# A conditioned transformer block on one core: sums and P7 issued later in a step, the second norm spread over four slots, other banks and buffers

## The chip, the cores and the metric

The kernel runs on one core of a Trainium2 chip. A core has five engines with queues of their own: TensorE (PE, matrix products), VectorE (DVE), ScalarE (ACT), GpSimd (POOL) and SyncE (SP), which here only issues DMAs. The metric is the device time of one execution in microseconds.

Before the change three runs took 2557.16, 2556.14 and 2556.53 us: the median is 2556.53 us.

## The reference

x is a tensor of 4 x 1024 tokens with 512 features, conditioned by a vector per sequence. In short (names as in the reference):

```python
def _tc_rmsnorm(x, t, gw, gb, bw, bb):
    g = (t @ gw.T + gb)[:, None, :]
    b = (t @ bw.T + bb)[:, None, :]
    inv_rms = jax.lax.rsqrt(jnp.mean(x * x, axis=-1, keepdims=True) + EPS)
    return g * x * inv_rms + b
...
# _attention: 16 heads of 32, softmax over 1024 keys, no mask
attn = jnp.einsum('blhd,bmhd->bhlm', q, k) / scale
p = jax.nn.softmax(attn, axis=-1)
o = jnp.einsum('bhlm,bmhd->blhd', p, v).reshape(B, L, D)
...
def _swiglu(x, gate_w, hid_w, out_w):      # 2048 hidden features
    return jax.nn.silu(x @ gate_w.T) * (x @ hid_w.T) @ out_w.T
...
h = x + _attention(_tc_rmsnorm(x, t, g1w, g1b, b1w, b1b), Wq, Wk, Wv, Wo)
block = h + _swiglu(_tc_rmsnorm(h, t, g2w, g2b, b2w, b2b), gate_w, hid_w, out_w)
return x + block
```

## The kernel before

Everything is float32 (the shift of the softmax travels in three bfloat16 parts). Features lie on the 128 partitions and tokens along the free axis. The 4096 tokens are 8 blocks (NBLK) of 512. Most products of PE are four at a time on 32 columns of weights each (`mm` with `columns[0] = DH`).

**Slots and rounds.** The main loop runs over slots g = 0 to 267. In slot g < 256 one round of attention begins: four heads, 256 queries and 256 keys (`scores`, L299). Four rounds (UN = 4) make one softmax j; `kind = g % 4` is the place in it. A round goes through the engines over several slots:
- `keep` copies the scores from their bank to SBUF on ACT (L306); `running_max` follows the maximum on DVE (L311).
- In a slot of kind 0, `max_T` and `parts` turn and reduce the maximum of the last four rounds; in kind 1 `parts_T` brings it back to rows (copy to mT on ACT, L338), and `spread` (L346) brings it to all keys: two products, each evicted by ACT to `shift`.
- `shifted` adds the shift (DVE, L352), `exponential` is on ACT (L355), `weighted` multiplies with the values (PE, L365, bank "av"), and `accumulate` adds the exponentials to one tile by a DMA on POOL's queue (L379).
- `fold_sum` (DVE) adds the two halves, `sums` (PE, L397) adds over the keys, `sums_out` copies the total (ACT, L406) and writes a compact form to DRAM (`compact`, L149, a DMA on ACT's queue). A step later `take` reads it as 128 x 8 numbers, `invert` takes the reciprocal, `put` (L165, ACT's queue) writes it back, and `sums_in` spreads it (SP's queue, L171). `normalize` multiplies.

**Feed-forward.** From g = 60 (FS) each slot pair also does half of a pass p = (g-60)//2: 128 hidden features of gate and of value for one block of 512 tokens. Gate and value products of one pass are made by a scheme with seven half-size products P1 to P7 (instead of eight) on sums of tokens (`token_sums`) and sums of weights (`weight_sums`, made in the first stage and kept in DRAM as s_w). P1 and P5 of the next pass are at the end of an odd slot (`pair_15`, `take_5`, `add_15`), P2 and P6 at the start of an even one (`pair_26`, then `copy_156`, L543, on ACT), then comes a **filling chain** (`filler`: the output product of an older pass, 32 matmuls of 512 columns, "pc"), P7 and `sub_5` (L550), in the next slot P3, the gate (`gate_tanh`, L560, `gate`), P4 and `hidden`. Passes 104 to 127 run in a tail loop behind slot 267.

**What sets the order.** On PE, DVE, ACT and POOL the order is that of the code. On SP, which issues most loads, a scheduler sets it. The first slots (g < 60) fill PE with projections from a queue of chains (`chain`), whose weights are loaded by `fetch` when the chain before is taken. A block of 32 slots (BS) also carries, for the block of tokens whose attention has ended: the load of the residual (slot 6 of a block, 1 MB), the output projections (slot 13 on, `project_out`, L443), the second norm (`norm_squares`, `norm_root`, the compact inverse by ACT's queue, `norm_scale`, `norm_mod`, L185, slots 15 to 25) and the token sums (25 to 27). These are hung into the loop by `after`, `between` and `amid` (end of a slot, before its end, in its middle).

**Banks and buffers.** PSUM: "sc" (scores), "av" (values), two of "w" (everything else), "wb" (bank_b of a pass). In SBUF tags that matter here: "fw" (4 buffers, weights of the projections and of the passes), "st" (2, staging of projected keys, queries and values once the token sums exist, and P5), "ow" (4, output weights), "inv", "tot", "rec".

Of the kernel before, what the change touches and what calls it, by code (L numbers as in the profile page):

```python
# [10 lines left out]
F32 = mybir.dt.float32  # L11
# [6 lines left out]
P = 128  # L18
NB = 512
# [5 lines left out]
def tile_cond_transformer_block(  # L25
# [24 lines left out]
    HQ = 256  # L50
# [52 lines left out]
    def mm(dst, w, moving, start: bool, stop: bool, seeded: bool = False):  # L103
        n = columns[0]
        for k in range(0, P, n):
            nc.tensor.matmul(  # L106
                dst[k : k + n, :], w[:, k : k + n], moving, start=start, stop=stop, skip_group_check=seeded
            )
# [4 lines left out]
    bank_a, bank_b, fifth = {}, {}, {}  # L113
    state = {}
    turn = [1]

    def bank(name: str):

        turn[0] += 1
        if "sums" not in state and turn[0] % 3 == 0:  # L120
            return ps_b.tile([P, NB], F32, tag="wb", name=name)
        return ps.tile([P, NB], F32, tag="w", name=name)
# [13 lines left out]
    def norm_root(tag: str, inside: bool = False):  # L136
        if inside:
            pm = ps_av.tile([P, NB], F32, tag="av", name=f"pm{tag}")
        else:
            pm = ps.tile([P, NB], F32, tag="w", name=f"pm{tag}")  # L140
        mm(pm, ones_mean, state.pop(tag), True, True)
        inv = sb.tile([P, NB], F32, tag="inv", name=f"inv{tag}", bufs=1)
        nc.scalar.activation(inv, pm, AF.Sqrt, bias=eps)
        state[tag] = inv

    def compact(tag: str, t, rows: int, n: int):

# [45 lines left out]
    def norm_sum(dst, tag: str):  # L193

        pm = ps.tile([P, NB], F32, tag="w", name=f"pm{tag}")
        for c in range(C):
            sq = sb.tile([P, NB], F32, tag="h", name=f"sq{tag}_{c}", bufs=7)
            nc.scalar.activation(sq, dst[:, c, :], AF.Square)
            nc.tensor.matmul(pm, ones_mean, sq, start=(c == 0), stop=(c == C - 1))
        inv = sb.tile([P, NB], F32, tag="inv" if tag == "a0_0" else "tot", name=f"inv{tag}", bufs=1)  # L200
        nc.scalar.activation(inv, pm, AF.Sqrt, bias=eps)
        nc.vector.reciprocal(inv, inv)
        state[tag] = inv
# [15 lines left out]
        y[b, half] = t  # L219

    def load_wkq(hg: int):
        t = sb.tile([P, 2, C, P], F32, tag="fw", name=f"wkq{hg}", bufs=4)
        nc.sync.dma_start(out=t, in_=kq_w[hg])
        wkq[hg] = t

    def staging(name: str):

        if "sums" in state:
            return sb.tile([P, NB], F32, tag="st", name=name, bufs=2)
        return sb.tile([P, NB], F32, tag="h", name=name, bufs=7)  # L230


# [234 lines left out]

    def weight_sums(f: int, step: int):
        if step == 0:
            state["gh", f] = sb.tile([P, 2, C, P], F32, tag="fw", name=f"gh{f}", bufs=4)  # L470
            nc.sync.dma_start(out=state["gh", f], in_=gh_w[f])
        else:
            t = state.pop(("gh", f))
            a11, a12, a21, a22 = (t[:, i, k : k + 2, :] for i in range(2) for k in (0, 2))
            o = sb.tile([P, 4, 2, P], F32, tag="fw", name=f"s{f}", bufs=4)
            nc.vector.tensor_tensor(o[:, 0], a21, a22, ALU.add)
            nc.vector.tensor_tensor(o[:, 1], o[:, 0], a11, ALU.subtract)
            nc.vector.tensor_tensor(o[:, 2], a11, a21, ALU.subtract)
            nc.vector.tensor_tensor(o[:, 3], a12, o[:, 1], ALU.subtract)
            nc.sync.dma_start(out=s_w[f], in_=o)  # L480
# [18 lines left out]

    def load_f(p: int, part: int):  # L500
        f = p % NF
        fw[p, part] = sb.tile([P, 4, 2, P], F32, tag="fw", name=f"fw{p}_{part}", bufs=4)
        if part == 0:
            nc.sync.dma_start(out=fw[p, 0][:, 0:2], in_=gh_w[f][:, 0].rearrange("p (a c) o -> p a c o", a=2))
            nc.sync.dma_start(out=fw[p, 0][:, 2:4], in_=s_w[f][:, 0:2])
        else:
            nc.sync.dma_start(out=fw[p, 1][:, 0:2], in_=s_w[f][:, 2:4])
            nc.sync.dma_start(out=fw[p, 1][:, 2], in_=gh_w[f][:, 1, 2:4])
# [11 lines left out]
        product(a[:, RIGHT], fw[p, 0][:, 2], state["sums"][:, 0])  # L520

    def take_5(p: int):
        fifth[p] = sb.tile([P, HQ], F32, tag="st", name=f"p5_{p}", bufs=2)
        nc.scalar.copy(fifth[p], bank_a[p][:, RIGHT])

    def add_15(p: int):
# [73 lines left out]
    def between(g, fn, *a):  # L600
        halfway.setdefault(g, []).append((fn, a))

    def after(g, fn, *a):
        ended.setdefault(g, []).append((fn, a))
# [40 lines left out]
    for n in range(NBLK):  # L645
        g0 = (n + 1) * BS
        pin(g0 + 6, load_res, n)
        go = g0 + (13 if n < NBLK - 1 else 8)
        for d in range(C):
            first.append((go, None, project_out, (n, d)))  # L650
            pin(go - 3 + (d // 2 * 4 if n else 0), load_wo, n, d)
        if n < NBLK - 1:
            tag = f"f{n}"
            after(g0 + 16, add_res, n)
            for k in range(2):
                after(g0 + 15 + k, lambda n=n, tag=tag, k=k: norm_squares(x2[n], tag, k))
            if g0 + 17 < FS:
                between(g0 + 17, norm_root, tag)
            else:
                amid.setdefault(g0 + 17, []).append((norm_root, (tag, True)))  # L660
            between(g0 + 17, norm_compact, tag)
            after(g0 + 19, take, tag)
            between(g0 + 20, invert, tag)
            after(g0 + 21, put, tag)
            after(g0 + 22, norm_spread, tag)
            for c in range(C):
                after(g0 + 24 + c // 2, lambda n=n, tag=tag, c=c: norm_scale(x2[n], tag, c))
                after(g0 + 24 + c // 2, lambda n=n, c=c: norm_mod(1, n // QB, x2[n], c))
            after(g0 + 25, token_sums, n, 0)
            for i in range(1, 3):  # L670
                after(g0 + 26, token_sums, n, i)
            between(g0 + 27, token_sums, n, 3)
    for m in range(NBLK * C):
        if m:
            for qh in range(NB // HQ):
# [8 lines left out]
    def fetch():  # L684

        if loads:
            load, a = loads.popleft()
            load(*a)
# [11 lines left out]
    with tc.manual_schedule(  # L700
# [6 lines left out]
        wv[0] = sb.tile([P, C, D], F32, tag="b", name="wv", bufs=2)  # L707
        nc.sync.dma_start(out=wv[0], in_=v_w)
        load_modw(1)
        fetch()  # L710
        norm_sum(y[0, 0], "a0_0")

# [28 lines left out]
        def filler(p: int, tail: bool = False):  # L741
# [15 lines left out]
                (lambda: take_contract(q, pp)),  # L757
            )

        while g < END:  # L760
            kind = g % UN
            r_x, r_v = g - UN - 1, g - UN - 2
# [31 lines left out]
            if v_on:  # L794
                weighted(r_v)
                accumulate(r_v)
            if kind == 0 and n_on:
                sums(j_n)
                if j_n >= direct:
                    inverse(j_n)  # L800
                    normalize(j_n)
            if kind == 1 and m_on:
                spread(j_m, 2)
                mT.pop(j_m)
# [1 line left out]
                shifted(r_x, slice(HG // 2, HG))  # L806
            if g < NR:
                keep(g)
            if kind == 0 and n_on and j_n < direct:
                sums_out(j_n)  # L810
            if kind == 1 and n_on and near(j_n) and j_n < direct:
                nc.vector.reciprocal(state["rec", j_n], state["rec", j_n])
            if kind == 2 and n_on and not near(j_n):
                take(f"s{j_n}")
            if kind == 0 and o_on and not near(j_o):
                put(f"s{j_o}")
            if kind == 1 and s_on:
                take_av(j_s)
            due = bool(first) and first[0][0] <= g
            if not ffn:  # L820
                if x_on:
                    exponential(r_x)
                evict = chain(g, FG)
                if g < NR:
                    running_max(g, 0)
                    running_max(g, 1)
# [21 lines left out]
            elif even:  # L848
                load_f(p + 1, 1)
                pair_26(p)  # L850
                copy_156(p)
                if x_on:
                    exponential(r_x)
                if kind == 0 and m_on:
# [7 lines left out]
                    running_max(g, 1)  # L862
                if evict is not None:
                    evict()
                if kind == 0:
                    pair_7(p)
                    sub_5(p)
                for fn, a in halfway.pop(g, []):
                    fn(*a)
            else:  # L870
                load_f(p + 2, 0)
                extra = due or len(queue) > FG
                if kind == 3:
                    if extra:
                        chain(g)()
                    pair_7(p)
                    sub_5(p)
                pair_3(p)
                if kind == 1 and extra:
                    chain(g)()  # L880
                if kind == 3:
                    gate_tanh(p)
                if x_on:
# [4 lines left out]
                    fn(*a)  # L888
                if kind == 1:
                    gate_tanh(p)  # L890
                if g < NR:
                    running_max(g, 0)
                if kind == 3:
                    gate(p)
                if g < NR:
# [1 line left out]
                add_15(p + 1)  # L897
                if kind == 1:
                    gate(p)
                if kind == 3 and s_on:  # L900
                    fold_sum(j_s)
                pair_4(p)
# [15 lines left out]
        assert not (pinned or amid or halfway or ended or queue or first)  # L918
        n = NBLK - 1
        squares = []  # L920
        for c, tag in enumerate(("rmax", "shift", "tot", "inv")):
            sq = sb.tile([P, NB], F32, tag=tag, name=f"sqf{n}_{c}", bufs=1)
            nc.scalar.activation(sq, x2[n][:, c, :], AF.Square)
            squares.append(sq)
# [84 lines left out]
```

## Time and profile before

| | us |
|---|---|
| median of three runs | 2556.53 |
| profiled execution | 2552.28 |
| its span | 2550.5 |
| PE busy | 2412.4 (95%) |
| DVE busy | 1853.8 (73%) |
| ACT busy | 1404.3 (55%) |
| DMA moved | 509.68 MB, mean 200 GB/s |

The page divides the span into forty slices of 63.8 us. DVE and ACT fall in the last five, in which the tail loop runs:

```profile
DVE  2677877766868887788788877888788868833332
ACT  3666767765656665665566556665565656512110
DMA  5598999998878998888788978899788978863442
```

In such a line a digit is the busy share of a slice in tenths. A row of the costliest groups has the line, the engine, output and inputs, how often it ran, and then its busy time, the mean of one in ns, and the idle time of its engine just before, with what ended it. In the timeline, a row shows start and duration in us, and in brackets how long the engine had idled before it and which instruction released it. [...] The mean granted clock of PE was 0.989 of full speed.

### The profile page before, as it was taken

Reading aid. Unit: us, or ns where it says so; the run is one execution under the profiler, and the core shown is the slowest. Engines: PE = TensorE matmul, PEld = TensorE weight load, DVE = VectorE, ACT = ScalarE, POOL = GpSimd, SP = SyncE. Lnnn points to the kernel's source line nnn. Section 1 sums busy time; section 2 is a strip of 40 time slices with the busy share of each in tenths; the row PEclk is TensorE's granted clock in tenths of the full one; section 3 lists DMA queues with packets and bytes.
Section 4 is the critical chain, followed back from the end, with each engine's and each line's share of the span. In section 5 each row is a group of like instructions: output and inputs, shape, how many; then the busy total and the mean of one; then the engine's idle time right before and its main releaser. Section 6 shows DMA issues by size and latency. Waiting matters only on the chain. (4 is left out here: it accounts for less than half of the span.)

```text
span 2550.5 us, 71967 instructions
## 1 busy us (share of the span) xinstructions
PE 2412.4 (95%) x31749; PEld 1137.8 (45%) x31749; DVE 1853.8 (73%) x2180; ACT 1404.3 (55%) x1486; POOL 172.4 (7%) x207
## 2 busy tenths in 40 slices
PE   8989999998999999999999999999999999989999
PEld 3333333344444444444444444454445444434444
DVE  2677877766868887788788877888788868833332
ACT  3666767765656665665566556665565656512110
POOL 0000000000000000000000000000000000000000
PEclk9999999999999999999999999999999999999999
DMA  5598999998878998888788978899788978863442
GB/s 200 162 260 244 249 239 250 239 219 197 190 183 205 220 224 193 197 207 219 190 207 205 224 189 201 195 228 219 184 202 216 225 182 202 199 159 116 138 126 90
DMA packets 245085, 509.68 MB, mean 200 GB/s; under 512 B 44483, under 2 KB 125471, under 8 KB 217382
## 3 DMA queue, kind: packets, MB, share of 16 engines
q0 software_dynamic: 28656, 208.68, 42.4%
q1 hardware_dynamic: 197520, 295.66, 35.8%
q8 instruction: 251, 4.11, 0.6%
q10 hardware_dynamic: 18598, 0.74, 0.5%
q14 instruction: 60, 0.49, 0.1%
HBM read 253.87 MB, written 42.42 MB: 116 GB/s over the span
## 5 line engine op out<-in xcount | busy, mean ns | idle before, releaser
L352 DVE TENSOR_TENSOR raw<-raw,shift 128x2048 f32<-128x2048 f32 (+1 forms) x320 | 592.7, 1853 | 120.9 <-ACT shift L347 115.8
L355 ACT ACTIVATE raw<-raw 128x2048 f32<-128x2048 f32 x256 | 490.7, 1917 | 120.2 <-DVE raw L352 84.9
L306 ACT COPY raw<-sc 128x2048 f32<-128x2048 f32 x256 | 479.3, 1872 | 136.4 <-PE sc L299 102.1
L311 DVE TENSOR_TENSOR rmax<-rmax,raw 128x1024 f32<-128x1024 f32 x384 | 468.4, 1220 | 60.2 <-ACT raw L306 54.7
L106 PE MATMUL pc<-h,ow 128*32 128x512 f32 x4096 | 467.9, 593 | 2.1 <-DVE rec L419 2.1
L106 PE MATMUL pa<-x,fw 128*32 128x256 f32 x6144 | 387.3, 384 | 9.5 <-DVE x L448 5.7
L365 PE MATMUL av<-raw,v 128*32 128x256 f32 x4096 | 277.9, 389 | 28.3 <-ACT raw L355 21.9
L379 POOL DMA_DIRECT2D raw<-raw x192 | 165.3, 861 | 2059.6 <-ACT raw L355 1014.5
L299 PE MATMUL sc<-q,k 32*128 32x256 f32 x4096 | 295.2, 402 | 1.0 <-ACT raw L306 1.0
L106 PEld LDWEIGHTS pa<-x,fw 128*32 128x32 f32 x6144 | 198.5, 111 | 161.4 <-issue 24.2
L106 PE MATMUL pa<-sums,fw 128*32 128x256 f32 x4096 | 270.3, 380 | 0.0
L106 PE MATMUL pkq<-y,wkq 128*32 128x512 f32 (+1 forms) x1664 | 236.0, 605 | 14.9 <-DMA wkq<-in_kq_w 10.8
L299 PEld LDWEIGHTS sc<-q,k 32*128 32x128 f32 x4096 | 185.9, 185 | 138.1 <-issue 86.5
L106 PEld LDWEIGHTS pc<-h,ow 128*32 128x32 f32 x4096 | 127.6, 110 | 246.1 <-issue 217.6
L543 ACT COPY pb<-pa 128x256 f32<-128x256 f32 x128 | 46.0, 359 | 246.8 <-PE pa L106 179.3
L365 PEld LDWEIGHTS av<-raw,v 128*32 128x32 f32 x4096 | 107.8, 110 | 154.5 <-ACT raw L355 49.0
L106 PEld LDWEIGHTS pa<-sums,fw 128*32 128x32 f32 x4096 | 138.1, 111 | 84.9 <-issue 2.0
L560 ACT ACTIVATE t<-pa 128x512 f32<-128x512 f32 x128 | 77.8, 608 | 157.6 <-PE pa L106 157.5
L581 DVE SCALAR_TENSOR_TENSOR res<-pc,res 128x512 f32<-128x512 f32 x128 | 88.1, 688 | 82.7 <-PE pc L106 82.7
L106 PE MATMUL pb<-x,fw 128*32 128x256 f32 x2048 | 134.1, 379 | 9.9 <-ACT pb L543 9.9
L106 PEld LDWEIGHTS pkq<-y,wkq 128*32 128x32 f32 (+1 forms) x1664 | 74.1, 119 | 146.5 <-issue 122.9
L106 PE MATMUL pb<-sums,fw 128*32 128x256 f32 x2048 | 134.1, 379 | 2.8 <-DVE pb L550 2.8
(103 smaller groups left out, 1930.0 us busy)
## 6 DMA issues: line engine op xcount, KB each, us to landing
raw<-raw POOLq DMA_DIRECT2D x192, 1024.0 KB, 8.9
fw<-sw SPq DMA_DIRECT2D x256, 256.0 KB
ow<-in_out_w SPq DMA_DIRECT2D x128, 256.0 KB
fw<-in_gh_w SPq DMA_DIRECT2D x128, 256.0 KB
wkq<-in_kq_w SPq DMA_DIRECT2D x32, 512.0 KB
v<-vs SPq DMA_DIRECT2D x128, 128.0 KB
fw<-in_gh_w SPq DMA_DIRECT2D x128, 128.0 KB
k<-kqs SPq DMA_DIRECT2D x124, 128.0 KB
```

Source lines behind the costliest of these rows:

```text
L106: nc.tensor.matmul(dst[k : k + n, :], w[:, k : k + n], moving, start=start, stop=stop, skip_group_check=seeded)
L299: nc.tensor.matmul(sc[:, i, k, :], keys[rows, k * P : (k + 1) * P], queries[rows, :], start=True, stop=True)
L306: nc.scalar.copy(raw[r].rearrange("p k h q -> p h k q"), state.pop(("sc", r)))
L311: nc.vector.tensor_tensor(rmax[j], rmax[j], raw[r][:, k, :, :], ALU.max)
L352: nc.vector.tensor_tensor(t, t, s.unsqueeze(1).to_broadcast(list(t.shape)), ALU.add)
L355: nc.scalar.activation(raw[r], raw[r], AF.Exp)
L365: nc.tensor.matmul(av[j][i * DH : (i + 1) * DH, :], v[m, u][:, k, i * DH : (i + 1) * DH], raw[r][:, k, i, :], start=(kt == 0), stop=(kt == ...
L379: nc.gpsimd.dma_start(out=acc[j].rearrange("p k h q -> p (k h q)"), in_=raw[r].rearrange("p k h q -> p (k h q)"), accum_op=ALU.add,)
L543: nc.scalar.copy(bank_b[p][:, RIGHT], bank_a[p][:, RIGHT])
L560: nc.scalar.activation(state["t", p], bank_a[p], AF.Tanh, scale=0.5)
L581: nc.vector.scalar_tensor_tensor(r, pp, 0.5, r, ALU.mult, ALU.add)
```

## The change

1. **Sums.** `sums`, `sums_out` and `put` move, in slots of kind 0, from before (and around) `keep` to a new function `take_sums`. In g < 60 it is called behind the exponential and the chain, from g = 60 on behind P2, P6 and the copy of pb, before the exponential.
2. **P7.** `pair_7` and `sub_5` follow the filling chain in slots of kind 0 and of kind 2; before, those of kind 2 came at the start of slot kind 3.
3. **Second norm.** `norm_scale` stays in slots 24 and 25. `norm_mod` of features 0 and 1 goes to the end of slot 25, of 2 and 3 to the middle of slot 26; the token sums to the ends of 26, 26, 27 and 28. The norm's total and inverse share one tile.
4. **Output projections** of kind 1 slots go behind P1, P5 and the gate's tanh into a bank of the tag "av" (`spare_bank`), and are evicted behind the gate. In kind 3 the chain stays ahead of P3, but is evicted behind the first running maximum.
5. **Weights.** "fw" has five buffers, and one more `fetch` at the start puts the loads of the projection weights two steps ahead. Staging uses the four buffers of "ow" once the token sums exist; P5 has a tag of its own with two.

The number of instructions on each engine is the same. The core of the diff:

```diff
+    spare_bank = [False]
 
     def bank(name: str):
 
+        if spare_bank[0]:
+            spare_bank[0] = False
+            return ps_av.tile([P, NB], F32, tag="av", name=name)
...
-        mm(pm, ones_mean, state.pop(tag), True, True)
-        inv = sb.tile([P, NB], F32, tag="inv", name=f"inv{tag}", bufs=1)
-        nc.scalar.activation(inv, pm, AF.Sqrt, bias=eps)
-        state[tag] = inv
+        mm(pm, ones_mean, state[tag], True, True)
+        nc.scalar.activation(state[tag], pm, AF.Sqrt, bias=eps)
...
     def load_wkq(hg: int):
-        t = sb.tile([P, 2, C, P], F32, tag="fw", name=f"wkq{hg}", bufs=4)
+        t = sb.tile([P, 2, C, P], F32, tag="fw", name=f"wkq{hg}", bufs=5)
...
         if "sums" in state:
-            return sb.tile([P, NB], F32, tag="st", name=name, bufs=2)
+            return sb.tile([P, NB], F32, tag="ow", name=name, bufs=4)
...
     def take_5(p: int):
-        fifth[p] = sb.tile([P, HQ], F32, tag="st", name=f"p5_{p}", bufs=2)
+        fifth[p] = sb.tile([P, HQ], F32, tag="p5", name=f"p5_{p}", bufs=2)
         nc.scalar.copy(fifth[p], bank_a[p][:, RIGHT])
...
                 after(g0 + 24 + c // 2, lambda n=n, tag=tag, c=c: norm_scale(x2[n], tag, c))
-                after(g0 + 24 + c // 2, lambda n=n, c=c: norm_mod(1, n // QB, x2[n], c))
-            after(g0 + 25, token_sums, n, 0)
-            for i in range(1, 3):
-                after(g0 + 26, token_sums, n, i)
-            between(g0 + 27, token_sums, n, 3)
+            for c in range(2):
+                after(g0 + 25, lambda n=n, c=c: norm_mod(1, n // QB, x2[n], c))
+            for c in range(2, C):
+                between(g0 + 26, lambda n=n, c=c: norm_mod(1, n // QB, x2[n], c))
+            for i in range(4):
+                after(g0 + (26, 26, 27, 28)[i], token_sums, n, i)
...
+        fetch()
         fetch()
...
+        def take_sums(j: int, j_before: int):
+
+            if 0 <= j < NR // UN:
+                sums(j)
+                if j >= direct:
+                    inverse(j)
+                    normalize(j)
+                else:
+                    sums_out(j)
+            if 0 <= j_before < direct and not near(j_before):
+                put(f"s{j_before}")
...
-            if kind == 0 and n_on:
-                sums(j_n)
-                if j_n >= direct:
-                    inverse(j_n)
-                    normalize(j_n)
...
-            if kind == 0 and n_on and j_n < direct:
-                sums_out(j_n)
...
-            if kind == 0 and o_on and not near(j_o):
-                put(f"s{j_o}")
...
                 evict = chain(g, FG)
+                if kind == 0:
+                    take_sums(j_n, j_o)
                 if g < NR:
                     running_max(g, 0)
...
                 pair_26(p)
                 copy_156(p)
+                if kind == 0:
+                    take_sums(j_n, j_o)
                 if x_on:
                     exponential(r_x)
...
-                if kind == 0:
-                    pair_7(p)
-                    sub_5(p)
+                pair_7(p)
+                sub_5(p)
...
             else:
                 load_f(p + 2, 0)
                 extra = due or len(queue) > FG
-                if kind == 3:
-                    if extra:
-                        chain(g)()
-                    pair_7(p)
-                    sub_5(p)
+                evict = None
+                if kind == 3 and extra:
+                    evict = chain(g)
                 pair_3(p)
-                if kind == 1 and extra:
-                    chain(g)()
                 if kind == 3:
                     gate_tanh(p)
                 if x_on:
@@ -888,8 +894,13 @@
                     fn(*a)
                 if kind == 1:
                     gate_tanh(p)
+                    if extra:
+                        spare_bank[0] = True
+                        evict = chain(g)
                 if g < NR:
                     running_max(g, 0)
+                if kind == 3 and evict is not None:
+                    evict()
                 if kind == 3:
                     gate(p)
                 if g < NR:
@@ -897,6 +908,8 @@
                 add_15(p + 1)
                 if kind == 1:
                     gate(p)
+                    if evict is not None:
+                        evict()
```

More of the change, by code (lines that the diff above doesn't have):

```diff
@@ L199, in norm_sum @@
             nc.tensor.matmul(pm, ones_mean, sq, start=(c == 0), stop=(c == C - 1))
-        inv = sb.tile([P, NB], F32, tag="inv" if tag == "a0_0" else "tot", name=f"inv{tag}", bufs=1)
+        inv = sb.tile([P, NB], F32, tag="rmax" if tag == "a0_0" else "tot", name=f"inv{tag}", bufs=1)
         nc.scalar.activation(inv, pm, AF.Sqrt, bias=eps)
@@ L469, in weight_sums @@
         if step == 0:
-            state["gh", f] = sb.tile([P, 2, C, P], F32, tag="fw", name=f"gh{f}", bufs=4)
+            state["gh", f] = sb.tile([P, 2, C, P], F32, tag="fw", name=f"gh{f}", bufs=5)
             nc.sync.dma_start(out=state["gh", f], in_=gh_w[f])
@@ L474, in weight_sums @@
             a11, a12, a21, a22 = (t[:, i, k : k + 2, :] for i in range(2) for k in (0, 2))
-            o = sb.tile([P, 4, 2, P], F32, tag="fw", name=f"s{f}", bufs=4)
+            o = sb.tile([P, 4, 2, P], F32, tag="fw", name=f"s{f}", bufs=5)
             nc.vector.tensor_tensor(o[:, 0], a21, a22, ALU.add)
@@ L501, in load_f @@
         f = p % NF
-        fw[p, part] = sb.tile([P, 4, 2, P], F32, tag="fw", name=f"fw{p}_{part}", bufs=4)
+        fw[p, part] = sb.tile([P, 4, 2, P], F32, tag="fw", name=f"fw{p}_{part}", bufs=5)
         if part == 0:
@@ L920, in tile_cond_transformer_block @@
         squares = []
-        for c, tag in enumerate(("rmax", "shift", "tot", "inv")):
+        for c, tag in enumerate(("rmax", "shift", "tot", "oT0")):
             sq = sb.tile([P, NB], F32, tag=tag, name=f"sqf{n}_{c}", bufs=1)
```

## The prediction

> **What bounds the kernel now.** I read the shares of the page first, then the forty slices, then the sums of waits, then the timeline around each wait of TensorE (PE).
>
> ```profile
> PE 2412.4 (95%) x31749; PEld 1137.8 (45%) x31749; DVE 1853.8 (73%) x2180; ACT 1404.3 (55%) x1486; POOL 172.4 (7%) x207
> PE   8989999998999999999999999999999999989999
> PEclk9999999999999999999999999999999999999999
> ```
>
> PE is busy for 2412.4 of 2550.5 us, in every slice. No product is removed by the change, so it can win only PE's idle time (138 us) and the half-clock stretches that follow idle time. I laid PE's rows on the order in which the code issues them and took, for each group, its start minus the previous start minus the usual length of the previous group (0.86 us for a product on 32 columns, 0.43 for the sums, 3.43 for a chain of 512 columns). What is over is lost. Per block of 32 slots it is 33.5, 25.8, 34.5, 23.6, 25.9, 26.7, 24.1, 25.3 us; some 0.2 to 0.6 us a slot of that comes with every change of shape and stays. These rows say who is waited for:
>
> ```profile
> L106 PE MATMUL pkq<-y,wkq 128*32 128x512 f32 (+1 forms) x1664 | 236.0, 605 | 14.9 <-DMA wkq<-in_kq_w 10.8
> ```
> ```profile
> ACT pb L543 <- DMA res<-in_x: 16.1, 2, 8.1
> PEld sum L397 <- issue: 38.6, 34, 7.5
> PE sum L397 <- issue: 20.9, 11, 7.0
> ```
>
> **Part 1, weights two steps ahead.** At t = 132.26 PE waited 6.14 us for a wkq load and then ran the chain at half clock (64 matmuls took 9.24 us where 2 x 3.64 are usual). The slot of g=10 and the two after it lost 6.33 + 2.2 + 1.2 us. With one fetch more and a fifth "fw" buffer this load is issued a whole step earlier: I take 8 of 9.7. g=38 loses 3.93 us to the next such load: 3.9. At g=20 ACT sits in an inverse's DMA until a load lands (3.98 us, then 2.6 in the next slots); the DMA still waits, but the exponential now goes ahead of it: 2.5. The fifth buffer adds no transfer, but lets loads of all stages start earlier, among others that share the 16 DMA engines, which are busy 8 to 9 tenths in most slices; a load that is early takes its share from one that is due. I count that at nothing and hold 3 us either way for it. Bounds 5 to 19, taken 14.4.
>
> **Part 2, the sums behind P2 and P6.** The sum's product waits for the fold on DVE, and everything of PE behind it in the slot. Of 49 slots in the mixed stage these waits make 32.2 us: 3.65 and 7.22 at g=64 and 68, (part 4), some 13 us in slots 20 and 28 of the blocks (about 1.0 and 1.4 each), 0.13 in the others. Behind P2 and P6 the fold has 1.7 us more (two products), so waits up to that go: per block 1.0 (slot 20) + 0.8 (the small ones); slot 28 is counted in part 3. For g < 60 the sum goes behind the 3.43 us chain: the 0.96, 0.7, 0.7, 0.39 and smaller waits there, 4 us. Near the end (g=256 to 264) the sums wait 0.8 to 4.3 us: 3 of it goes. What moves to ACT: total (0.37), compact and put (0.5 and 0.3 to 0.4 us as issues) now stand between the copy of pb and the exponential, 1.2 us later for the exponential. ACT idles about 3.4 us before the mT copy in that slot, so it is hidden.
>
> It is not hidden where one of those DMAs waits. Each DMA on ACT's queue waits for the one that last used its completion semaphore (8 lanes, dealt in the order of building). In slot 4 of a block, that was in the trace the 1 MB residual:
>
> ```profile
> 1172.30 0.32 ACTq L165 DMA_DIRECT2D invss<-fews  x1
> 1172.66 0.36 ACT L543 COPY pb<-pa 128x256 f32<-128x256 f32 x1 [7.99 <-DMA res<-in_x]
> 1172.93 1.91 ACT L355 ACTIVATE raw<-raw 128x2048 f32<-128x2048 f32 x1
> 1173.07 1.07 PE L106 MATMUL pb<-x,fw 128*32 128x256 f32 x16 [2.75 <-ACT pb L543]
> ...
> 1174.74 0.34 ACT L338 COPY mT<-pt 12x256 bf16<-12x256 bf16 x1
> ...
> 1176.14 0.63 PE L346 MATMUL sp<-mT,select 12*128 12x256 bf16 x2
> ```
>
> ACT stands still for 8 us, and PE loses 2.75 us in P7. After the change the copy of pb is ahead, so P7 no longer waits. But the dealing shifts: put now follows the query load that is queued right behind the residual. These land at 908.0, 1176.2, 1445.9, 1715.1 and 1982.2 us in the trace; put went at 903.0, 1172.3, 1441.5, 1709.9 and 1977.3. Queued behind put on ACT are the exponential (1.91) and mT (0.34), and PE's spread waits for mT: it comes at landing + 0.35 + 1.91 + 0.35 + 0.1 = landing + 2.7, where it was put + 2.85 before (0.77 to P7, 0.86, 0.25, 0.97). So 4.5 us a block are lost more, 22.7 in five blocks, though P7's stall goes. PE then idles 6.7 us at a stretch (spread possible at 1172.2, comes at 1178.9).
>
> Here a rule bears. **The Trainium skill, "TensorE: Matmul & The Clock Gate", Part 1**: PE falls to half clock after about one idle window of 3.4 us, and gets the full clock back after a busy window. By it each 6.7 us stall costs one window at half speed, 1.7 us. The trace agrees only in part: 1.9 us of idle time was enough in slot 25, and 3.93 us at g=38 were not followed by a slow stretch. The nearest row is g=68, 7.2 us idle and then 0.4 + 0.84 + 1.03 + 0.64 = 2.9 us lost. By the rule 8.5 us, by the row 14.5, less 1.5 that slot 4 loses this way now: 7 or 13. I take 10. Slot 4: -33 (ends: 0 if the load lands early, -45).
>
> **Part 3, P7 behind the filling chain, and the norm over four slots.** In slot 25 mT stands behind two norm_mods on ACT:
>
> ```profile
> 1346.91 1.52 ACT L185 ACTIVATE x<-x,mod 128x512 f32<-128x512 f32 x2 [4.31 <-DVE x L182]
> 1348.34 0.34 ACT L338 COPY mT<-pt 12x256 bf16<-12x256 bf16 x1
> 1348.73 0.37 PE L346 MATMUL sp<-mT,select 12*128 12x256 bf16 x2 [1.72 <-ACT mT L338]
> ```
>
> They move to the end of slot 25 and the middle of 26, the token sums to 26 to 28. Gone: 1.9 in slot 25, 0.67 to 1.1 and 0.75 in 27 (P4 behind sub_5, which P7's place mends), 1.41 in 28: 4.4 to 5.2. The same DVE work lies now later, beside shifted (2.23), running_max (2 x 1.22) and the take_contract: I charge 1.3 for the exponential in 28 and up to 0.6 for P2, net 3.3. Four of six blocks have a half-clock stretch behind slot 25 (0.6 to 1.5): 0.7 a block on average. P7 moved by a step costs PE nothing, its inputs lie there; it waits for the copy of pb, issued a 3.43 us chain earlier.
>
> **Part 4, banks and buffers.** Output projections in the values' bank: slot 13 waited 1.03 + 1.0 us for DVE to empty the shared bank; av is idle then: 2.0 a block. The new bank could hold back the next av; that product is a step later, and the eviction (0.69) stands ahead: nothing, at worst 0.7 a block. That the second norm's total and inverse share one tile costs nothing: the root waits for the product that reads the total as it did. Staging moves from "st" to "ow" and take_5 gets its own tag:
>
> ```profile
> 627.37 0.37 ACT L524 COPY p<-pa 128x256 f32<-128x256 f32 x1 [7.17 <-DMA vs<-sv]
> ```
>
> Removed: 3.65 + 7.22 + 1.38 waits and 2.9 half clock = 15.2. New: the first output weights now wait for staging's stores; by the landings of the trace ow0 comes about 3.4 us after its first chain could start, and put and compact in that slot wait for ow2 and ow3. I charge 6; net 9 (ends 0 to 15).
>
> **The sum.** Blocks: 2.0 + 1.0 + 0.8 + 3.3 + 0.7 = 7.8, times 6 = 47. Then 18 (14.4 + 4) + 9 + 47 + 3 - 33 = 44. The profiled execution took 2552.28 us around a span of 2550.5; that is 4.25 us less than the median of the runs, 2556.53. 2552.3 - 44 = 2508, and with those 4 us **2512**.
>
> **Rivals.**
> - *The query load lands early* (PE is faster, the queue of SP gets its buffers sooner), so slot 4 loses nothing: 44 + 33 = 77, 2480. For it: SP's order is the scheduler's. Against it: the load stands behind 1 MB in all five blocks. 0.12.
> - *DVE becomes the bound.* It is at 8 tenths in most slices of the mixed stage. Then what is won in slots 13 and 24 to 28, 6 x (2.0 + 3.3 + 0.7) = 36, is lost again a step later: all of it gives 44 - 36 = 8 (2549), half of it 26 (2530). I put it at half, 2530. Against it: DVE's waits for PE and ACT (115.8 us for shift alone) are slack that later work can use. 0.2.
> - *The blocked ACT queue decides* (slower): compact and put in slot 4, in all blocks, wait for the residual and what follows it, and spread waits for them. All else gives 77, so it decides from 15.4 us a block (five blocks) or 11 (seven); put stood still for 8 us already now, but behind work that hid 5 of it. At 13 in seven blocks (8 more than now, and a block's half-clock stretch with it) it takes 91 from the 77: 2480 + 91 = 2571. 0.1, and 0.04 for an end within the bound of no change.
> - *The change doesn't do what it says* (the scheduler puts the loads back where they were, so part 1 gives nothing): 2526. It is inside the range, with the forecast in its 0.54.
>
> **How the numbers follow.** The likeliest is 2512, its own range 2496 to 2528. The range for 8 in 10 takes in DVE as a bound and half of the early load: 2488 to 2546. A difference under 0.2% (5 us) can't be told from none. Faster 0.86, same 0.04, slower 0.10.
>
> **What would show it.** Right: no wait for wkq at g=10; no wait of ACT's p for vs; in slot 25 spread at once behind sc; in slot 4 P7 without a wait, but spread waiting for mT some 6 us, and behind it a slow clock. Wrong: slot 4 without that wait (then about 2480), or av and P2 waiting for exponentials in slots 26 to 30 (DVE).

## The result and the profile after

The changed kernel takes 2525.52 us (median of four runs, 2524.23 to 2529.8), the kernel before 2556.34 us beside it: a ratio of 0.9884, with an interval of 0.9867 to 0.9901. That is 30.8 us or 1.2% faster; 44 us were forecast. The profiled execution of the changed kernel took 2529.8 us around a span of 2528.0 us, so it is the slowest of its four, and the spans of the two traces differ by 22.5 us only. What follows is summed against those 22.5.

First the page after: the shares of the engines, the clock and the row of the projections.

```profile
PE 2404.4 (95%) x31749; PEld 1131.5 (45%) x31749; DVE 1854.4 (73%) x2180; ACT 1409.2 (56%) x1486; POOL 172.8 (7%) x207
...
PEclk9999999999999999999999999999999999999999
...
L106 PE MATMUL pkq<-y,wkq 128*32 128x512 f32 (+1 forms) x1664 | 231.6, 594 | 6.6 <-ACT y L187 4.1
```

PE's idle time before the projections fell from 14.9 to 6.6 us, and loads no longer lead it. The mean granted clock, though, fell from 0.989 to 0.986: there is more half-clock time than before. The sums of waits after the change say where (waiting engine and line, what released it, us in total, times, longest):

```profile
ACT raw L357 <- DMA sumss<-total: 79.7, 19, 15.4
...
PE sp L348 <- ACT mT L340: 49.1, 8, 11.3
...
PEld sum L399 <- issue: 8.1, 23, 1.6
...
PE pma L106 <- ACT total L408: 4.7, 5, 1.7
```

PE's weight loads for the sums wait 8.1 us where it was 38.6, and the copy of pb no longer waits for the residual (16.1 us before). In their place stands a wait of 79.7 us on ACT, behind the issue of the compact sums, and PE waits 49.1 us for the mT copy in front of spread. This is slot 4 of a block, in the timeline of the changed kernel (start, duration, row; in brackets idle time before it, and releaser):

```profile
1141.17 0.33 SPq L435 DMA_DIRECT2D res<-in_x  x1
...
1141.59 0.39 SPq L290 DMA_DIRECT2D v<-vs  x1
1142.03 0.42 SPq L285 DMA_DIRECT2D q<-kqs  x1
...
1145.62 1.05 PE L106 MATMUL pb<-x,fw 128*32 128x256 f32 x16
...
1146.82 1.15 PE L301 MATMUL sc<-q,k 32*128 32x256 f32 x16
...
1153.41 0.50 ACTq L151 DMA_DIRECT2D sumss<-total  x1
1154.01 0.40 ACTq L167 DMA_DIRECT2D invss<-fews  x1
1154.45 1.91 ACT L357 ACTIVATE raw<-raw 128x2048 f32<-128x2048 f32 x1 [12.80 <-DMA sumss<-total]
1156.27 0.34 ACT L340 COPY mT<-pt 12x256 bf16<-12x256 bf16 x1
...
1156.66 0.58 PE L348 MATMUL sp<-mT,select 12*128 12x256 bf16 x2 [8.70 <-ACT mT L340]
```

P7 (the pb row) goes without a wait, as forecast. The total was there at 1141.65, but compact could be issued only at 1153.41. The trace records which semaphore a DMA raises and which an instruction waits for: compact waits for the one that the value load (issued 1141.59) raises, and put for that of the query load. Both loads stand behind the 1 MB residual, and by the records the last of their parts landed at 1153.34 and 1153.52. ACT takes its queue in order: the exponential has had its input from DVE since 1141.78 and starts at 1154.45, 0.04 us after put's issue ends. PE is idle from 1147.96 to 1156.66. What follows it is this table of stretches (their times and length, busy us of PE, PEld, DVE, ACT and POOL with counts, then granted clock, DMA share and GB/s):

```profile
1137.00:1147.00 10.00, 10.00 (x134) 4.96 (x138) 8.72 (x14) 2.71 (x4) 0.86 (x1) 1.00 0.70 181
1147.00:1156.60 9.60, 0.96 (x16) 0.63 (x16) 0.24 (x1) 2.15 (x2) 0.00 (x0) 0.81 0.91 251
1156.60:1163.40 6.80, 6.74 (x60) 2.71 (x63) 3.75 (x4) 4.32 (x6) 0.86 (x1) 0.52 0.94 169
1163.40:1170.00 6.60, 6.60 (x112) 3.43 (x104) 6.37 (x7) 4.63 (x6) 0.00 (x0) 1.00 0.61 193
```

In the 6.8 us after the stall the mean clock is 0.52. In finer stretches it is 0.50 from 1152.88 to 1163.12 and 1.00 just before and behind: PE is idle for the first 3.8 us of that and then works at half clock for 6.5 us, where the forecast had one window of 3.4 us.

The account by stage, from the start of one slot's scores to the next in both traces:

| stage | forecast, us | traces, us |
|---|---|---|
| ahead of slot 0 | 0 | +1.0 |
| slots 0 to 59 | -18 | -11.6 |
| slots 60 to 71 | -9 | -10.6 |
| slots 4 to 7 of five blocks | +33 | +10.9 +6.7 +6.3 +8.8 +9.5, in all +42.3 |
| all other slots from 72 to 251 | -47 | -40.0 |
| from slot 252 to the end | -3 | -3.6 |
| sum | -44 | -22.5 |

### The profile page after: what moved, and what is told of

Same layout as the page of the kernel before. It is cut to its first block, busy times and chain, and to the rows that moved or that the text cites. A ratio compares the mean times of both kernels' runs of the same rounds, so it can differ in the third digit from the quotient of the medians.

```text
span 2528.0 us, 72020 instructions
## 1 busy us (share of the span) xinstructions
PE 2404.4 (95%) x31749; PEld 1131.5 (45%) x31749; DVE 1854.4 (73%) x2180; ACT 1409.2 (56%) x1486; POOL 172.8 (7%) x207
## 5 line engine op out<-in xcount | busy, mean ns | idle before, releaser
L106 PEld LDWEIGHTS pa<-x,fw 128*32 128x32 f32 x6144 | 193.1, 111 | 166.4 <-issue 30.5
```

The lines of the kernel that those rows point to most:

```text
L106: nc.tensor.matmul(dst[k : k + n, :], w[:, k : k + n], moving, start=start, stop=stop, skip_group_check=seeded)
```

## The experiments

The theory was that ACT is held in slot 4 by two DMAs of its own that wait for loads queued behind the residual, and that everything else of the change is worth some 65 to 75 us. The rivals: that the two issues cost ACT this time wherever they stand, and that the loss came with PE's earlier arrival, not with the sums.

**The residual held back.** One line in the changed kernel: DVE writes one column of the residual's buffer at slot 6, and the load has to follow it. Compact and put still wait for the query and the value load, though in exchanged order.

```diff
         res[n] = sb.tile([P, C, NB], F32, tag="b", name=f"res{n}", bufs=2)
+        nc.vector.memset(res[n][:, 0, 0:1], 0.0)
         nc.sync.dma_start(out=res[n], in_=x[n])
```

> The changed kernel, but the 1 MB residual load is held back until slot 6 of its block (a one-column memset on DVE that the load has to follow), so that it no longer stands ahead of the value and query loads in slot 4. Compact and put on ACT's queue still wait for the same two loads as in the changed kernel. Theory (ACT is held in compact and put by loads that are queued behind the residual): these land some 3 us after their issue, the 8 to 11 us wait of spread for mT goes in all five blocks, and with it the half clock behind it; slots 4 and 5 lose 61 us over five blocks now, so about 2470 us (2465 to 2480, if the later residual delays one weight load a block by 2 to 3 us). Rival 1 (the wait is the price of issuing two DMAs on ACT ahead of the exponential, whatever loads there are): 2525, as the changed kernel. Rival 2 (the stall only moves to slot 6, where the weights now stand behind the residual): 2500 to 2525.

Measured: 2477.09 us, ratio 0.9692 (0.9672 to 0.9713). The same place in its timeline:

```profile
1135.65 0.37 ACT L408 COPY total<-sum 128x256 f32<-128x256 f32 x1
1136.05 0.50 ACTq L151 DMA_DIRECT2D sumss<-total  x1
...
1136.65 0.40 ACTq L167 DMA_DIRECT2D invss<-fews  x1
1137.09 1.91 ACT L357 ACTIVATE raw<-raw 128x2048 f32<-128x2048 f32 x1 [1.07 <-DMA sumss<-total]
```

Compact goes 0.03 us after the total is there. From the start of the total to the exponential it is 1.4 us, where the changed kernel has 13.2. Slots 4 and 5 together lose 2.1 us a block (mean of six) instead of 11.6. In five of the six blocks they lose just the usual 0.7 us, in the first 9.3. Rival 1 of this run falls: the two issues stand where they stood. Its rival 2 (the stall only moves to slot 6) falls as well: slot 6 loses 0.7. This version beats both kernels, by 3.1% and, against the changed one, by some 1.9%.

Why the loads are there in time shows on SP's queue. In the changed kernel the residual itself waits, for the store out of its old buffer, and SP stands still for it. SP's waits there from 1130 to 1143 us include:

```profile
SPq L435 <- DMA out<-res: 8.7, 1, 8.7
```

The value and query loads, next in the queue, went out 4.7 and 5.1 us after the start of the slot's scores. With the residual held back they went out 3.3 and 4.3 us before it (the scores of this slot start at 1131.28):

```profile
1126.95 0.33 SPq L285 DMA_DIRECT2D q<-kqs  x1
1127.95 0.59 SPq L290 DMA_DIRECT2D v<-vs  x1
```

They took 7.9 (value) and 8.6 us (query) from issue to the last landing, not the 3 us that the expectation had, and 11.8 and 11.5 us in the changed kernel. So of the 12 us by which they land earlier in the slot, 8 to 9.5 are their earlier issue and 3 to 4 the shorter way. In the five blocks of both kernels the later of the two landed 0.2 to 1.1 us after a 1 MB accumulation of POOL's queue; no run moved that one, so whether it sets the landing is not shown.

That first block with feed-forward (its slot 4 is g=68) is the check. There SP was late for another reason, a store of staging, and with no residual ahead the two loads went out 3.7 and 4.6 us after the scores. The stall came all the same:

```profile
611.26 0.77 SPq L285 DMA_DIRECT2D q<-kqs  x1
612.12 0.47 SPq L290 DMA_DIRECT2D v<-vs  x1
...
619.55 0.50 ACTq L151 DMA_DIRECT2D sumss<-total  x1
...
621.60 1.91 ACT L357 ACTIVATE raw<-raw 128x2048 f32<-128x2048 f32 x1 [9.32 <-DMA v<-vs]
...
623.81 0.58 PE L348 MATMUL sp<-mT,select 12*128 12x256 bf16 x2 [5.21 <-ACT mT L340]
```

**Compact and put behind mT.** Here the residual stays first and the two DMAs move, one slot later on ACT: they wait in a list, of which this part of the edit takes them.

```diff
+            while kind == 1 and waiting:
+                fn, a = waiting.pop(0)
+                fn(*a)
             if kind == 1 and s_on:
                 take_av(j_s)
```

> The changed kernel, but from g=60 on compact and put are issued one slot later, on ACT behind the copy of the scores of kind 1 (behind mT and both shift copies); the sum and the copy of the total stay where the change put them. Theory (mT and spread stand behind ACT's two waiting DMAs): spread no longer waits; ACT is still held till the loads land, but 4 to 5 us later in the order, which costs 0 to 2 us a block: 2465 to 2480 us. Rival (ACT's slack is used up, so that the exponential of slot 5 comes late instead): 2500 or more.

Measured: 2511.78 us, ratio 0.9835 (0.9803 to 0.9867). The number is the rival's. Slot 5 loses 0.3 us, as the theory had it, but slot 6 loses 5.6:

```profile
1152.52 0.50 ACTq L151 DMA_DIRECT2D sumss<-total  x1
1153.96 0.32 ACTq L167 DMA_DIRECT2D invss<-fews  x1
1154.32 0.37 ACT L393 COPY avs<-av 128x256 f32<-128x256 f32 x1 [3.92 <-DMA k<-kqs]
1154.59 1.91 ACT L357 ACTIVATE raw<-raw 128x2048 f32<-128x2048 f32 x1
...
1156.56 1.20 PE L367 MATMUL av<-raw,v 128*32 128x256 f32 x16 [3.88 <-ACT raw L357]
```

Put is issued 18.5 us after the start of the scores of slot 4, where the changed kernel has 17.1, and now the next exponential is late, which av waits for. But the move also changed what the two DMAs wait for. The semaphores are dealt in the order of building, and by the records compact now waits for a weight load (last part at 1152.44) and put for a key load (1153.94). ACT had come to compact at 1150.41, and the value and query loads had landed at 1150.69 and 1151.05. So this run does not show what the move alone is worth, nor that ACT has no slack in slot 5; with the old loads the hold would have been under 1 us in this slot (an estimate from these times).

**The first part undone from g=60 on.** `sums`, `sums_out` and `put` of the mixed stage go back to their old places around the copy of the scores; the rest is as changed.

```diff
+            if ffn and kind == 0 and n_on:
+                sums(j_n)
...
                 copy_156(p)
-                if kind == 0:
-                    take_sums(j_n, j_o)
```

> The changed kernel with its first part undone from g=60 on (sums ahead of the copy of the scores, total, compact and put ahead of P2's copy of pb), all else as changed. Theory: put then waits for the residual itself, as before the change, which P7 pays with about 3 us a block and some half clock (20 us in five blocks), and the sums wait for the fold again (2 to 2.5 us a block, 13); the 61 us of slots 4 and 5 go: 2525 - 61 + 20 + 13 = 2497 us. So this part is a loss in this stage. Rival (behind P2 and P6 is worth more than it costs): above 2525.

Measured: 2507.58 us, ratio 0.9814 (0.9788 to 0.984), 18 us faster than the whole change. In its sums of waits the residual is back in front of the copy of pb, as in the kernel before:

```profile
ACT pb L545 <- DMA res<-in_x: 22.4, 3, 8.0
```

So in this stage the first part cost more than it won. Of the 10 us above the expectation, slot 28 has a part: it loses 3.5 us (1.9 before, 2.5 after), since the early sum waits for a fold on DVE, where the norm and token sums have moved. Slot 6 has another, 1.5 us where both other kernels lose 0.2.

**The first part alone.** The kernel before with `take_sums` and nothing else.

> The kernel before with the first part alone (sums, total, compact and put later in slots of kind 0). Theory: the stall of spread comes as in the changed kernel (12.5 us in slots 4 and 5 of five blocks, where the kernel before loses about 3): +46; the sums no longer wait for the fold: -15; nothing in the first stage, where a bank is held longer: 2556 + 31 = 2587 us. By the sizes of the prediction (33 lost, 18 won): 2571. Rival (the stall comes only together with the other parts, since they bring PE sooner to slot 4): 2540.

Measured: 2581.52 us, ratio 1.0085 (1.0055 to 1.0115): slower by 0.85%. Slots 4 and 5 lose 10.9 us a block where they lost 4.4. The stall needs no other part of the change, and PE's earlier arrival is not its cause.

**The later sums without the obstacle.** Both: the residual held back, and the first part undone from g=60 on.

> The changed kernel with the residual held back and the first part undone from g=60 on. It tells what the later sums are worth in the mixed stage once nothing stands ahead of compact and put. Theory (the sums' waits for the fold are 1.0 to 1.5 us in slots 20 and 28 and 0.1 to 0.3 elsewhere): 2477 + 6 x 2.5 = 2492. Rival (DVE's slack takes it, the sums' place is worth nothing): 2477.

Measured: 2489.45 us, ratio 0.9744 (0.9721 to 0.9768), that is 12.4 us above the run with the residual held back alone. The move of the sums is worth 12 us when nothing holds ACT; slots 20 and 28 carry it (1.8 against 0.5, 3.8 against 2.5).

**The residual held back in the kernel before.** The same added line, in the kernel before.

> The kernel before with nothing but the residual held back until slot 6. Theory: put no longer waits for the residual, so P7 of slot 4 doesn't wait for the copy of pb; slots 4 to 7 lose some 4.5 us a block less: 2555 - 23 = 2532 (up to 2540, if the later load delays weights in slot 7). Rival (what was hidden stays hidden, and the load costs elsewhere): 2555.

Measured: 2531.31 us, ratio 0.99 (0.9872 to 0.9928). This one line alone wins nearly as much as the whole change.

**The other parts alone.** The fifth (weights and buffers), then the second and third together (P7, norm), each put into the kernel before as the change has it.

> The kernel before with the fifth part alone (fifth weight buffer, one more fetch, staging in the output weights' buffers, a tag of its own for P5; the norm's total and inverse share one tile, to make room). By the prediction 14.4 + 9 us: 2532. By the changed kernel's trace (11.6 us won ahead of g=60, of which the run with the sums alone had 2.5, and 10.6 from 60 to 72): 2555 - 20 = 2535. Rival (the early wins were the sums' and not the weights'): 2543 or more.

Measured: 2539.37 us, ratio 0.9932 (0.9909 to 0.9955): 17 us, where 20 and 23 were expected. Its trace wins 10.4 us in slots 60 to 71 but only 2.9 ahead of slot 60: 5.4 at g=10 and 4.0 at g=38 are won, and among the losses are 4.0 at g=55, a slot that differs by -0.8 to +2.8 us from the kernel before in three runs whose code is the same up to there. Slot 7 loses 1.3 us a block more than before.

> The kernel before with parts two and three alone (P7 of kind 2 behind the filling chain, the second norm over four slots). By the prediction (3.3 + 0.7) x 6 = 24 us: 2531. By the changed kernel's trace, slot 25 wins 2.9, slot 27 1.3, slot 28 loses 0.6: 3.6 x 6 = 22, 2533. Rival (DVE becomes the bound in slots 26 to 30 and takes it back): 2545 or more.

Measured: 2532.25 us, ratio 0.9899 (0.9868 to 0.993). Slot 25 loses 0.3 us instead of 3.2, slot 27 0.2 instead of 1.5, slot 7 0.2 instead of 1.3; slot 28 loses 4.2 instead of 1.9, of which 1.55 us are the sum behind the fold. In the changed kernel slot 28 loses 2.5, since there the sum has moved: the parts help each other.

The fourth part (output projections in the values' bank):

> The kernel before with the fourth part alone (output projections of kind 1 in the values' bank, evicted behind the gate). By the prediction 2.0 us in slot 13 of six blocks: 2543. By the changed kernel's trace (1.9 in slot 13, 0.6 in slot 12): 2540. Rival (the values' bank holds back the next av, or the win is swallowed in the next slot): 2552 or more.

Measured: 2553.92 us, ratio 0.999 (0.9972 to 1.0007): no change that can be told. It did win 1.9 us in slot 13, but slot 15 lost 1.8. Its timeline there:

```profile
1268.39 1.05 PE L106 MATMUL pb<-x,fw 128*32 128x256 f32 x16
1269.25 1.05 PE L106 MATMUL pa<-x,fw 128*32 128x256 f32 x16
1269.57 0.43 DVE L554 TENSOR_TENSOR pb<-pb,p 128x256 f32<-128x256 f32 x1 [3.55 <-PE pb L106]
1269.91 1.21 DVE L315 TENSOR_TENSOR rmax<-rmax,raw 128x1024 f32<-128x1024 f32 x1
...
1271.04 0.68 DVE L452 TENSOR_TENSOR x<-po,res 128x512 f32<-128x512 f32 x1
...
1271.83 1.07 PE L106 MATMUL pa<-x,fw 128*32 128x256 f32 x16 [1.53 <-issue]
```

DVE had been idle for 3.55 us, but its queue starts with the subtraction that needs P7. Behind it come the running maximum and only then the eviction of the output projection (L452, done at 1271.72). P1 of the next pass, which takes one of the two "w" banks, starts 0.1 us later. If that is the cause, P7 a step earlier must mend it:

```diff
-                if kind == 0:
-                    pair_7(p)
-                    sub_5(p)
+                pair_7(p)
+                sub_5(p)
```

> The kernel before with the fourth part and P7 of kind 2 behind the filling chain. Theory (alone, the fourth part wins 1.9 us in slot 13 and gives back 1.8 in slot 15, where P1 waits for a bank that DVE empties only behind a running maximum, which itself stands behind the subtraction after P7): with P7 a step earlier the wait in slot 15 goes, and P4's in slot 27: (1.9 + 0.3 + 1.3) x 6 = 21, 2537. Rival (slot 15 waits for something else): 2547 or more.

Measured: 2531.89 us, ratio 0.9905 (0.9873 to 0.9938). Slot 15 loses 0.4, slot 13 0.5. So the fourth part needs the second (which was not run by itself).

**The total ahead of the exponential in the first stage.** In the changed kernel, for g below 60, the copy of the total stands on ACT behind an exponential, and the norm's product waits for the bank of the sum:

```profile
146.94 1.91 ACT L357 ACTIVATE raw<-raw 128x2048 f32<-128x2048 f32 x1 [2.68 <-DVE raw L354]
...
148.76 0.35 ACT L408 COPY total<-sum 128x256 f32<-128x256 f32 x1
...
149.17 1.13 PE L106 MATMUL pma<-tota,ones_mean 128*128 128x512 f32 x2 [1.68 <-ACT total L408]
```

The core of the edit, on top of the residual held back (with True, compact and put go into a list):

```diff
-                if x_on:
+                if kind != 0 and x_on:
                     exponential(r_x)
                 evict = chain(g, FG)
                 if kind == 0:
-                    take_sums(j_n, j_o)
+                    take_sums(j_n, j_o, True)
+                    if x_on:
+                        exponential(r_x)
+                    while waiting:
+                        fn, a = waiting.pop(0)
+                        fn(*a)
```

> The changed kernel with the residual held back (as in that run) and, for g below 60, the copy of the total ahead of the exponential on ACT, with compact and put still behind it. Theory (in the first stage the sum's bank is freed late, since the copy of the total stands behind the exponential, and the norm's product waits for that bank: 1.85, 0.36, 1.82, 0.36 and 1.17 us in the changed kernel's trace): 4 to 5 us less than the run with the residual held back, 2472. Rival (the exponential comes late instead, and av waits for it): 2477 or more. A difference of 5 us is at the edge of what the times tell; the trace's waits behind the transposed maximum tell it.

Measured: 2475.05 us, ratio 0.9692 (0.967 to 0.9715): no difference to the run it is compared with. The waits for that bank are gone from its trace, all five, so what they waited for is shown. The time is not won: slots 28 and 29 lose 2.3 and 1.8 us behind the projections instead, where ACT, behind compact and put, was idle for 4.43 us before it could evict one. Which of the orders is best there stays open.

## Why the prediction came out as it did

**The sign and the mechanism against it were right, and the size of that mechanism was short.** By the traces 12 us less were won than forecast and 9 more lost. The forecast named slot 4, put behind the query load, P7 free and spread waiting. The rival "the query load lands early" was priced at 2480 us, and when the residual was made to stand aside the kernel took 2477. Two terms of that step were mis-sized:
- PE's idle stretch: 6.7 us forecast, 8.4 to 11.5 measured. I had taken the landings of the query load from the trace of before, and read them too early: a load lands in sixteen parts, the times given lie in their middle, and put waits for the last, at 908.8, 1178.0, 1446.7, 1716.7 and 1984.4 by the semaphore records, 0.8 to 2.2 us later. In the slot shown, put goes 14.9 us after the start of the scores by the forecast, 16.8 with the right landing, and 17.1 in the trace after. The residual itself was issued 1 us later in the slot. That compact waits too, for the value load, was not in the forecast; in three of the five blocks it held ACT for nearly the whole time.
- The clock behind it: I took 2 us a block, between the rule's 1.7 and the row's 2.9. The slot shown above loses 12.1 us, of which 8.88 are the stall and 0.3 its usual loss: 2.9 us are left for the clock. In the five blocks PE worked for 6.0, 6.5, 6.1, 6.5 and 4.0 us at 0.50 behind the stall, of which half is lost, 2.9 us on average. The row was right. The forecast had read the rule of the Trainium skill ("TensorE: Matmul & The Clock Gate", Part 1) as one window of 3.4 us; the page says at least one busy window, and that the windows run free of the kernel, so up to nearly two can pass at half clock (an estimate from its figure: 1.7 to 3.4 us lost). The five stalls agree with that.

**Slots 0 to 59: 11.6 for 18.** The step that failed is "for g < 60 the sum goes behind the chain: 4 us", counted without the bank. The copy of the total moved behind the exponential too, the sum's bank came free later, and five norm products lost 1.85, 0.36, 1.82, 0.36 and 1.17 us, 5.6 in all (4.7 of it in the trace's row of waits). The weights two steps ahead won 5.8 at g=10, where I took 8: the second chain of that slot still waits 2.43 us for its load. g=38's 3.9 us went as forecast. The 11.6 are also one execution's: two other runs with the same code in these slots won 7.3 and 9.3 us by their traces, two with only the residual held back 8.9 and 9.3, and the sums alone 2.5.

**Slots 60 to 71: 10.6 for 9.** P5's own buffer took its waits away. The new wait for the first output weights came as forecast, at 2.50 us where 3.4 were reckoned.

**The steady blocks.** Slot 13 won 1.9 (2.0 forecast), slot 20 1.0 (1.0), slot 25 2.9 (1.9, and 0.7 for the clock), slot 27 1.3; slot 28 loses 0.6 more, where a gain of 1.4 and a charge of 1.3 had been set against each other. DVE did not become the bound: this rival had 0.2. Right by chance was the independence of the parts. Part 4 was priced by itself at 12 us, and by itself it gives nothing; it needs P7's new place, and slot 28 needs the sums'. From slot 252 on 3.6 us went, for 3.

## What to carry to other kernels

A DMA issued by a compute engine is an instruction with waits of its own; here a completion semaphore shared with SP's loads was enough to hold ACT for 12.8 us. Before moving such an issue ahead of work on the critical path, look up which earlier DMA it waits for, what is queued ahead of that one, and what that in turn waits for: here SP stood 8.7 us before the residual. To take the bulk load out of the way gave 2477 us; to move the waiter gave 2512, but it then waited for other loads, so look that up again after each move. Price the parts of a change in pairs where they share an in-order queue or a bank: the fourth part was worth nothing alone.

## What the runs showed of the hardware

- PE worked at a granted clock of 0.50 for 4.0 to 6.5 us after each of five stalls of 8.3 to 11.3 us in the changed kernel.
- A load of 128 KB took 7.9 to 8.6 us from issue to its last landing with no residual ahead of it (slot 4 of one block), and 11.5 to 11.8 us right behind the 1 MB residual. That ACT then waited 0.03 us instead of 11.8 came mostly from the issue, 8 to 9.5 us earlier in the slot.
